# Two-layer graph network on one core: a bias row loaded later, two combines moved, and the last product banks paired anew

## The chip, the cores and the metric

The kernel runs on one core of a Trainium2 chip. The metric is the device time of one execution in microseconds. The time before is the median of three runs. Engines are named as in the profile: PE (matmul) with its weight loads PEld, DVE (vector), ACT (scalar), POOL and SP. SP and POOL issue nearly all DMAs; each issues its own in program order, and an instruction that waits holds up all that stand behind it on its engine.

## What is computed

Input x has 4096 rows of 512 columns, and adj is a 4096 x 4096 integer matrix with about one entry in 128 set. The reference, cut to what matters:

```python
# layer 0: the first 64 neighbours of each row are averaged
keep    = Ab & (cumsum(Ab, axis=1) <= 64)
nb_mean = (keep @ x) / maximum(cnt, 1)
x1 = layernorm(x + leaky_relu(x @ W_line.T + b_line)
                 + where(cnt > 0, leaky_relu(nb_mean @ W_nb.T + b_nb), 0))
# layer 1: attention over the neighbours
wh  = x1 @ W + bW
e   = leaky_relu((wh @ a1 + b1)[:, None] + (wh @ a2 + b2)[None, :], 0.2)
att = softmax(where(adj > 0, e, -9e15), axis=1)
out = layernorm(x1 + att @ wh)
```

## The kernel before, in words

Rows are worked on in 32 blocks of 128. The tile framework sets the waits between engines, but the order of the instructions on each engine is the order in which the program writes them (`tc.manual_schedule()`). A reader can thus follow each engine's queue in the code.

**Layer 0** ends with the neighbour sums: for each of 32 blocks, 64 matmuls (L509, two terms for each of 32 column blocks) into one PSUM bank. The block before is finished meanwhile by DVE in four steps, `finish(i, 0)` to `finish(i, 3)` (L468 to L487): bias and leaky relu, the sum with `own` (the rest of x1, loaded from DRAM), the layer norm with the store of x1 to DRAM, and two dot products for the attention scores. The last block, 31, is finished after the last matmul.

**Between the layers** the memory of layer 0 is reused. Three tiles `w` of 16 KB a partition are taken for layer 1. The first, `front`, holds the weights `ws` and four slots `x1s` for x1 as it is loaded. The second, `early`, takes the first three transposed blocks of x1, scratch of `finish(31)`, and own of block 31. Further up, over memory that holds the operands of layer 0's matmuls, lie `bt`, the tile `res` with the bias row `bias_w`, and the buffers `nat` of packed adjacency. Program order on SP is: four loads of `ws` (L542), the bias row broadcast to 128 partitions (L546, 256 KB), `load_turned(0..3)`, own of block 31 (L777), eight loads of `nat` for block 0 (L608), `load_turned(4..6)`. On DVE it is: `turn_x1(0..2)`, then `finish(31)`, then some small sums (L788 to L794) that POOL sends through DRAM as `e2_n` and `st_n`, which the masks need.

**The squares of wh.** For s from 0 to 31, PE makes `wh` for 128 rows with four matmuls (L809). Ahead of that, `load_turned(s)` loads x1 in four DMAs (L561) and `turn_x1(s)` transposes it in blocks of 32 on DVE (L575). The loop runs three transpositions and seven loads ahead. A load waits for the transposition that frees its slot. `finish_wh(s)` (L584) adds the bias row and writes a half of `bt`. From s = 8 (`FIRST`) on, the loop also works on the attention weights of blocks 0 and 1: `mask` (ACT L621, DVE L624), `score` (ACT L613), the largest logit (`greatest`, `shift`), and `weigh` (ACT exp, L666). Late in the loop `turn(q)` (DVE, two instructions at L685) transposes a quarter of the weights of two blocks, and `combine(q)` (four DVE sums, L698 to L701) makes the sums that a Strassen-like scheme with seven products needs. `combine_wh` (four DVE sums, L597 to L600) does this for one pair of halves of `bt`. There are 16 such pairs. The loop calls it at each s from 16 on, except at s = 22 and 26; what is left is done while the first product group runs.

**The products.** For q from 0 to 63, `consume(q)` multiplies quarter k = q mod 4 of two row blocks g = q div 4 by `bt`: seven products of four matmuls each (L724), 12.09 us a quarter. The seven results of one g lie in four PSUM tiles of one bank each, two to a bank and one alone; `where` says which. Meanwhile DVE and ACT prepare `turn` and `combine` of the next quarters and the weights of the next blocks. After a g is done, `end_low` and `end_top` add the products and `end_row` adds x1, normalizes and stores. For the last g this is written out at the end of the program: ACT copies product 1, then DVE adds 6, 2, 7, 5, 4 and 3 in this order of reading (L877 to L889). In the very last quarter the order of the products is (4, 1, 2, 6, 7, 5, 3).

Of the kernel before, what the change touches and what calls it, by code (L numbers as in the profile page):

```python
# [20 lines left out]
P = 128  # L21
# [11 lines left out]
def two_layer_adj_gnn(  # L33
# [16 lines left out]
    nc = tc.nc  # L50
# [3 lines left out]
    NT = NB // 2  # L54
# [22 lines left out]
    two, steep, far, neg_half = few[:, 0:1], few[:, 1:3], few[:, 3:4], few[:, 4:5]  # L77
# [59 lines left out]
    with ExitStack() as l0:  # L137
# [325 lines left out]
        def finish(i, g):  # L463
            if i < 0:
                return
            if g == 0:
                t = place("t")
                nc.vector.scalar_tensor_tensor(  # L468
                    t, accs.pop(i), rcnt[:, i : i + 1], bias_nb, ALU.mult, ALU.add
                )  # L470
                nc.vector.scalar_tensor_tensor(t, t, 0.01, t, ALU.mult, ALU.max)  # L471
                fin[i] = t
            elif g == 1:
                t, y = fin[i], owns.pop(i)
                nc.vector.scalar_tensor_tensor(  # L475
                    y, t, some[:, i : i + 1], y, ALU.mult, ALU.add
                )
                fin[i] = y, ln_stats(y)
            elif g == 2:
                y, stats = fin[i]  # L480
                ln_apply(y, stats)
                nc.gpsimd.dma_start(x1_blk(i), y)
            else:
                y, _ = fin.pop(i)
                for k in range(2):
                    junk = place("junk", 1)
                    nc.vector.scalar_tensor_tensor(  # L487
                        junk, y, 1.0, wa_rows[k], ALU.mult, ALU.mult,
                        accum_out=e12[:, 1 - k, i : i + 1],
                    )  # L490
# [3 lines left out]
        for s in range(NB * NS):  # L494
            i, g = divmod(s, NS)
# [10 lines left out]
            for k in range(KB):  # L506
                j = g * KB + k
# [25 lines left out]
    NP = 4  # L533
# [9 lines left out]
            ws[ts(n, SQ), :, :], w[ts(n, P), :].rearrange("(m b) c -> b m c", b=SQ)  # L543
        )
    bias_w = ep.tile([P, C], F32, name="res", bufs=1)
    nc.sync.dma_start(bias_w, b_w.partition_broadcast(P))  # L546


    bt = big.tile([P, NS // 2, 7, HC], F32, name="bt")
# [6 lines left out]
    def load_turned(s):  # L556

        if s < NS:
            part = x1_d[s // 8].rearrange("(n s a) c -> s a n c", s=8, a=SQ)[s % 8]
            for n in range(NC):  # L560
                nc.sync.dma_start(  # L561
                    x1s[ts(n, SQ), s % 4, :].rearrange("a (j c) -> a j c", c=P),
                    part[:, :, ts(n, P)],
                )

    x1ts, x1rows, pws, nats, wts, parts = {}, {}, {}, {}, {}, {}
    m4s, mms, nms, z4s, zqs, rzs, banks, sums = {}, {}, {}, {}, {}, {}, {}, {}

    FIRST = 8

    def turn_x1(s):
        if s < NS:
            t = early[:, s, :C] if s < 3 else rows.tile([P, C], F32, name="c")
            x1ts[s] = t.rearrange("p (m i) -> p m i", i=P)
            nc.vector.transpose(  # L575
                x1ts[s].rearrange("p m (j a) -> p j m a", a=SQ),
                x1s[:, s % 4, :].rearrange("p (j m b) -> p j m b", m=NC, b=SQ),
            )

    def finish_wh(s):  # L580

        kk, h = s // 8 * 4 + s % 4, s // 4 % 2
        b = bt[:, kk]
        nc.vector.tensor_tensor(  # L584
            b[:, 2 * h : 2 * h + 2, :], pws.pop(s).rearrange("p (h c) -> p h c", h=2),
            bias_w.rearrange("p (h c) -> p h c", h=2), ALU.add,
        )
        if h == 1:
            later.append(kk)
# [12 lines left out]
    def load_nat(b, h):  # L602

        if b < NB:
            nats[b, h] = ep.tile([P, 2, NS * SQ // 2], BF16, name="nat")
            rows = code_d[b].rearrange("(i a) (n x) -> n a i x", a=SQ, n=4)
            for n in range(4):
                nc.sync.dma_start(nats[b, h][ts(n, SQ)], rows[n][:, ts(h, 2), :])  # L608
# [6 lines left out]
    def mask(b, i):  # L615

        if i == 0:
            wts[b] = early if b == 0 else wp.tile([P, NI, NS * SQ], F32, name="w")
            m4s[b] = stat.tile([P, NI], F32, name="m4", bufs=2)
        w_i = wts[b][:, i, :]  # L620
        nc.scalar.activation(  # L621
            w_i, nats[b, i // 2].bitcast(U8)[:, i % 2, :], AF.Relu, bias=far, scale=-FAR
        )
        nc.vector.tensor_tensor_reduce(  # L624
            w_i, e2_n, w_i, 1.0, -3e38, ALU.subtract, ALU.max, m4s[b][:, i : i + 1]
        )
        if i % 2:
            load_nat(b + 1, i // 2)

    def score(b, i):  # L630
        w_i = wts[b][:, i, :]
        bend1(b, i, w_i, w_i)
# [16 lines left out]
    def shift(b):  # L649


        mm = mms.pop(b)
        lm = stat.tile([P, NI], F32, name="lm", bufs=2)
        for i in range(NI):
            bend1(b, i, lm[:, i : i + 1], mm[:, i : i + 1])
        nms[b] = stat.tile([P, NI], F32, name="nm", bufs=2)
        nc.vector.scalar_tensor_tensor(  # L657
            nms[b], lm, -1.0, st_n[:, :, 1, b], ALU.mult, ALU.subtract
        )
# [20 lines left out]
    def turn(q):  # L680

        g, k = divmod(q, NP)
        a = rp.tile([P, 2, 8, P], F32, name="a")
        for r in range(2):
            nc.vector.transpose(  # L685
                a[:, r].rearrange("p s (i a) -> p i s a", a=SQ),
                wts[2 * g + r][:, :, ts(k, 8 * SQ)].rearrange("p i (s x) -> p i s x", x=SQ),
            )
        if k == NP - 1:
            del wts[2 * g], wts[2 * g + 1]  # L690
        parts[q] = a

    def combine(q):
        a = parts[q]
        s = rp.tile([P, 3, 4, P], F32, name="s")
        a11, a12, a21, a22 = a[:, 0, 0:4], a[:, 0, 4:8], a[:, 1, 0:4], a[:, 1, 4:8]
        s1, s2, s4 = s[:, 0], s[:, 1], s[:, 2]
        nc.vector.tensor_tensor(s1, a21, a22, ALU.add)  # L698
        nc.vector.tensor_tensor(a21, a11, a21, ALU.subtract)
        nc.vector.tensor_tensor(s2, s1, a11, ALU.subtract)  # L700
        nc.vector.tensor_tensor(s4, a12, s2, ALU.subtract)  # L701

        parts[q] = {
            1: (a11, 0), 2: (a12, 2), 3: (s4, 3), 4: (a22, 6), 5: (s1, 4), 6: (s2, 5), 7: (a21, 1)
        }


    where = {1: (0, 0), 2: (0, 1), 4: (1, 0), 7: (1, 1), 5: (2, 0), 6: (2, 1), 3: (3, 0)}

    def consume(q):  # L710
        g, k = divmod(q, NP)
        if k == 0:
            two = [ps_s.tile([P, 2, HC], F32, name="pt")]
            two += [ps_acc.tile([P, 2, HC], F32, name="acc") for _ in range(3)]
            banks[g] = {n: two[i][:, j, :] for n, (i, j) in where.items()}
        part = parts.pop(q)


        order = (1, 2, 4, 7, 5, 6, 3) if q < NP * NT - 1 else (4, 1, 2, 6, 7, 5, 3)
        for n in order:  # L720
            lhs, rhs = part[n]
            mate = [m for m in order if where[m][0] == where[n][0]]
            for j in range(4):
                nc.tensor.matmul(  # L724
                    banks[g][n], lhs[:, j, :], bt[:, 4 * k + j, rhs, :],
                    start=(k == 0 and j == 0 and n == mate[0]),
                    stop=(k == NP - 1 and j == 3 and n == mate[-1]),
                )
# [46 lines left out]
    for s in range(4):  # L775
        load_turned(s)
    nc.sync.dma_start(owns[NB - 1], own_d[NB - 1])  # L777
    load_nat(0, 0)
    load_nat(0, 1)
    for s in range(3):  # L780
        turn_x1(s)
        load_turned(s + 4)
    for g in range(4):
        finish(NB - 1, g)

# [19 lines left out]
    for s in range(NS):  # L805
        pws[s] = ps_acc.tile([P, C], F32, name="acc")
        x1t = x1ts.pop(s)
        for m in range(NC):
            nc.tensor.matmul(  # L809
                pws[s], x1t[:, m, :], ws[:, m, :], start=(m == 0), stop=(m == NC - 1)  # L810
            )
        if s > 0:
            finish_wh(s - 1)
        turn_x1(s + 3)
        load_turned(s + 7)
        if FIRST <= s < FIRST + 8:
            b, i = divmod(s - FIRST, NI)
            mask(b, i)
            score(b, i)
        if FIRST + 4 <= s < FIRST + 12:  # L820
            b, i = divmod(s - FIRST - 4, NI)
            if i == 0:
                greatest(b)
                shift(b)
            weigh(b, i)
        if s in (FIRST + 14, FIRST + 18):
            q = (s - FIRST - 14) // 4
            turn(q)
            combine(q)
        elif s >= FIRST + 8:  # L830
            combine_wh()
    finish_wh(NS - 1)

    for q in range(NP * NT):
        g, k = divmod(q, NP)
        consume(q)
        more = 0 < q < NP * NT - 1
        if more:
# [92 lines left out]
```

## Time and profile before

| what | value |
|---|---|
| runs | 1611.77, 1612.21, 1615.34 us, median 1612.21 |
| profiled execution | 1611.63 us, of which the span is 1609.9 |
| PE / DVE / ACT / POOL busy | 98% / 82% / 56% / 16% of the span |
| layer 0's last matmul ends | 704.21 us |
| squares of wh on PE | 709.69 to 826.06 us |
| products on PE | 826.06 to about 1599.6 us |
| work after the last matmul | about 10 us |

Times in the text count from the start of the span. PE's matmul records have modelled ends and overlap by a fraction of a microsecond, so stretches of PE are best measured from start to start. In the waits, a line says which instruction waited, which one released it, the total in us, how often, and the longest. In the timeline, `x24` means that neighbouring equal instructions are merged into one row; each matmul on 32-bit data leaves two records there.

### The profile page before, as it was taken

The page shows a single profiled execution, that of the slowest core. Times are in us where ns is not written, and L with a number is a line of the kernel's source. Part 1 is how long each engine was busy: PE and PEld are TensorE (multiplying, and loading weights), DVE is VectorE, ACT ScalarE, POOL GpSimd, SP SyncE. Part 2 cuts the span into 40 slices and gives each one's busy share as a digit, 9 for nine tenths or more (in the row PEclk, how much of TensorE's full clock was granted, in tenths as well). Part 3 has the DMA queues.
Part 4 walks back from the last instruction along what each step waited for, and adds up shares of the span by engine and source line. Part 5 has one row for each costly group of instructions (what it writes and reads, how often), then busy time and mean ns, then how long its engine had stood idle before and what let it go on. Part 6 is the DMA issues. An engine that isn't in the chain of part 4 may idle for free.

```text
span 1609.9 us, 18503 instructions
## 1 busy us (share of the span) xinstructions
PE 1583.8 (98%) x6456; PEld 1221.9 (76%) x6456; DVE 1328.1 (82%) x2186; ACT 903.2 (56%) x1054; POOL 258.1 (16%) x396
## 2 busy tenths in 40 slices
PE   9999999999999999989999999999999999999997
PEld 5444448888888787854468888888888888888886
DVE  4999987999999999845798788888788888788863
ACT  2655556677676766413437655567655567655520
POOL 4455532222122222101000000000000000000000
PEclk9999999999999999999999999999999999999999
DMA  8887868767776676335211111111111111111100
GB/s 199 286 264 232 262 211 239 216 202 212 220 208 198 209 213 193 100 103 118 79 40 27 53 40 53 44 29 46 53 41 53 43 30 47 53 40 53 40 7 33
DMA packets 168365, 192.74 MB, mean 120 GB/s; under 512 B 101408, under 2 KB 134464, under 8 KB 160080
## 3 DMA queue, kind: packets, MB, share of 16 engines
q1 hardware_dynamic: 147968, 131.38, 29.6%
q0 software_dynamic: 19728, 59.27, 10.8%
q8 instruction: 50, 0.82, 0.2%
q10 hardware_dynamic: 576, 0.92, 0.2%
q14 instruction: 43, 0.35, 0.1%
HBM read 132.65 MB, written 42.08 MB: 109 GB/s over the span
## 4 chain that ended last, share of the span: by engine, by line
PE 69%; DVE 23%; DMA 3%; issue 2%; ACT 1%; POOL 1%; SPq 0%; DVEq 0%; POOLq 0%; ACTq 0%
PE acc L724 34%; PE pt L724 14%; DVE left L179 10%; PE acc L340 9%; PE acc L509 9%; PE acc L809 3%; DVE left L184 2%; DVE junk L487 2%; DVE own L475 1%; DVE st L117 1%; DVE t L471 1%; DMA a<-in_adj_dram 1%; DVE t L468 1%; DVE own L131 1%; DVE c L575 1%
## 5 line engine op out<-in xcount | busy, mean ns | idle before, releaser
L509 PE MATMUL acc<-y_hi,kt 128*128 128x512 f32 x1016 | 396.3, 390 | 2.9 <-ACT kt L249 2.9
L509 PE MATMUL acc<-y_lo,kt 128*128 128x512 f32 x1016 | 395.8, 390 | 0.0
L724 PE MATMUL acc<-bt,s 128*128 128x256 f32 x1536 | 342.1, 379 | 0.0
L724 PEld LDWEIGHTS acc<-bt,s 128*128 128x128 f32 x1536 | 292.3, 190 | 39.2
L621 ACT ACTIVATE w<-nat,few 128x1024 f32<-128x1024 uint8 x128 | 136.9, 1135 | 277.1 <-DVE a L685 237.0
L126 POOL TENSOR_TENSOR rs<-ve,few 128x1 f32<-128x1 f32 x64 | 76.1, 1190 | 1021.1 <-DVE ve L124 1021.1
L724 PE MATMUL acc<-bt,a 128*128 128x256 f32 x1024 | 231.6, 379 | 0.0
L724 PE MATMUL pt<-bt,a 128*128 128x256 f32 x1024 | 231.5, 379 | 0.0
L509 PEld LDWEIGHTS acc<-y_hi,kt 128*128 128x128 f32 x1016 | 190.7, 188 | 44.5 <-ACT kt L249 5.0
L509 PEld LDWEIGHTS acc<-y_lo,kt 128*128 128x128 f32 x1016 | 190.9, 188 | 39.3
L724 PEld LDWEIGHTS pt<-bt,a 128*128 128x128 f32 x1024 | 194.9, 190 | 26.5 <-issue 0.5
L724 PEld LDWEIGHTS acc<-bt,a 128*128 128x128 f32 x1024 | 194.9, 190 | 26.1
L685 DVE STREAM_TRANSPOSE a<-w 128x1024 f32<-128x1024 f32 x128 | 153.0, 1225 | 56.1 <-ACT w L666 53.2
L249 ACT ACTIVATE kt<-ktb,few 128x1024 fp32r<-128x1024 uint8 x124 | 139.8, 1148 | 84.7 <-PE acc L509 69.0
L167 ACT ACTIVATE edge<-a,few 128x2048 bf16<-128x2048 int32 x64 | 127.9, 1998 | 99.4 <-DVE left L184 78.0
L613 ACT ACTIVATE w<-w,st_n 128x1024 f32<-128x1024 f32 x128 | 149.4, 1234 | 49.8 <-DVE m L624 49.8
L624 DVE CUSTOM_DVE_ANT_0 w<-e_n,w 128x1024 f32<-128x1024 f32 x128 | 149.5, 1221 | 9.1 <-ACT w L621 7.7
L666 ACT ACTIVATE w<-w,nm 128x1024 f32<-128x1024 f32 x128 | 145.4, 1137 | 11.3 <-DVE nm L657 11.3
L179 DVE TENSOR_TENSOR_SCAN left<-few,edge 128x2048 bf16<-128x2048 f32 x32 | 141.3, 4416 | 12.3 <-ACT edge L167 11.2
L179 DVE TENSOR_TENSOR_SCAN left<-few,ends,edge 128x2048 bf16<-128x2048 f32 x32 | 143.2, 4476 | 0.0
L202 ACT CAST code<-left 128x2048 uint8<-128x2048 bf16 x64 | 120.6, 1884 | 7.6 <-DVE left L184 7.6
L340 PE MATMUL acc<-wt_nb,xt 128*128 128x512 f32 x256 | 115.4, 594 | 1.8 <-DVE xt L294 1.0
(135 smaller groups left out, 1528.5 us busy)
## 6 DMA issues: line engine op xcount, KB each, us to landing
a<-in_adj_dram SPq DMA_DIRECT2D x64, 1024.0 KB, 5.7
code_d<-code POOLq DMA_DIRECT2D x64, 256.0 KB, 5.2
nat<-code_d SPq DMA_DIRECT2D x256, 64.0 KB, 2.0
own_d<-xb POOLq DMA_DIRECT2D x32, 256.0 KB, 5.7
w<-x_d SPq DMA_DIRECT2D x128, 64.0 KB, 2.0
c<-in_x_dram POOLq DMA_DIRECT2D x124, 64.0 KB, 5.5
xb<-in_x_dram POOLq DMA_DIRECT2D x31, 256.0 KB, 5.7
own<-own_d SPq DMA_DIRECT2D x31, 256.0 KB, 2.7
```

What stands on the lines that cost most here:

```text
L167: nc.scalar.activation(edge_of[s], loaded.pop(s), AF.Sigmoid, bias=steep[:, 0:1], scale=STEEP, accum_out=cnts[:, h, b : b + 1],)
L179: nc.vector.tensor_tensor_scan(left, two.to_broadcast([P, CH]), e, NEIGHBORS + 2.0 if h == 0 else end, ALU.max, ALU.subtract,)
L202: nc.scalar.copy(code.bitcast(U8), seen_of.pop(s))
L249: nc.scalar.activation(kts[s], bytes_.rearrange("p t (i r) -> p t r i", r=2), AF.Sigmoid, bias=steep[:, 1:2], scale=STEEP,)
L340: nc.tensor.matmul(pl, lhs_t[:, k, :], w_t[name][:, k, :], start=(k == 0), stop=(k == NC - 1),)
L509: nc.tensor.matmul(accs[i], kt[:, k // 2, k % 2, :], term[:, j, :], start=(j == 0 and term is y_hi), stop=(j == NB - 1 and term is y_lo),)
L613: nc.scalar.activation(dst, src, AF.Prelu, bias=bias, scale=scale, alpha=0.2)
L621: nc.scalar.activation(w_i, nats[b, i // 2].bitcast(U8)[:, i % 2, :], AF.Relu, bias=far, scale=-FAR)
L624: nc.vector.tensor_tensor_reduce(w_i, e2_n, w_i, 1.0, -3e38, ALU.subtract, ALU.max, m4s[b][:, i : i + 1])
L666: nc.scalar.activation(w_i, w_i, AF.Exp, bias=nms[b][:, i : i + 1], accum_out=z4s[g][:, r, i : i + 1])
L685: nc.vector.transpose(a[:, r].rearrange("p s (i a) -> p i s a", a=SQ), wts[2 * g + r][:, :, ts(k, 8 * SQ)].rearrange("p i (s x) -> p i s x ...
L724: nc.tensor.matmul(banks[g][n], lhs[:, j, :], bt[:, 4 * k + j, rhs, :], start=(k == 0 and j == 0 and n == mate[0]), stop=(k == NP - 1 and ...
```

## The change

The bias row's load moves from ahead of all x1 loads to behind `load_turned(6)`, and the eight `nat` loads of block 0 move behind `load_turned(7)`. In the squares' loop, `turn(0)`, `combine(0)`, `turn(1)` and `combine(1)` now stand at s = 22, 24, 26 and 28; before, each turn and its combine stood together at 22 and 26. At each of these four no `combine_wh` is called, so that four of the 16 instead of two are left to the first product group. For the last g, all four quarters use the order (4, 1, 2, 6, 7, 5, 3), and the banks hold (4, 1), (2, 6), (7, 5) and (3); before they held (1, 2), (4, 7), (5, 6) and (3) for every g. On PE, POOL and ACT nothing else changes its place.

```diff
     bias_w = ep.tile([P, C], F32, name="res", bufs=1)
-    nc.sync.dma_start(bias_w, b_w.partition_broadcast(P))
...
-    where = {1: (0, 0), 2: (0, 1), 4: (1, 0), 7: (1, 1), 5: (2, 0), 6: (2, 1), 3: (3, 0)}
+    order = {True: (1, 2, 4, 7, 5, 6, 3), False: (4, 1, 2, 6, 7, 5, 3)}
+    where = {key: {n: divmod(i, 2) for i, n in enumerate(o)} for key, o in order.items()}
...
-            banks[g] = {n: two[i][:, j, :] for n, (i, j) in where.items()}
+            banks[g] = {n: two[i][:, j, :] for n, (i, j) in where[g < NT - 1].items()}
...
-        order = (1, 2, 4, 7, 5, 6, 3) if q < NP * NT - 1 else (4, 1, 2, 6, 7, 5, 3)
-        for n in order:
+        key = g < NT - 1
+        for n in order[key]:
             lhs, rhs = part[n]
-            mate = [m for m in order if where[m][0] == where[n][0]]
+            mate = [m for m in order[key] if where[key][m][0] == where[key][n][0]]
...
     nc.sync.dma_start(owns[NB - 1], own_d[NB - 1])
-    load_nat(0, 0)
-    load_nat(0, 1)
     for s in range(3):
         turn_x1(s)
         load_turned(s + 4)
+    nc.sync.dma_start(bias_w, b_w.partition_broadcast(P))
     for g in range(4):
         finish(NB - 1, g)
...
         turn_x1(s + 3)
         load_turned(s + 7)
+        if s == 0:
+            load_nat(0, 0)
+            load_nat(0, 1)
...
-        if s in (FIRST + 14, FIRST + 18):
-            q = (s - FIRST - 14) // 4
-            turn(q)
-            combine(q)
+        if s in range(FIRST + 14, FIRST + 22, 2):
+            q, part = divmod((s - FIRST - 14) // 2, 2)
+            (turn, combine)[part](q)
         elif s >= FIRST + 8:
             combine_wh()
```

## The prediction

> **What bounds the kernel now.** I read the page first, then PE's waits, then the timeline and a table of windows around the one long wait, then the end. The page says whose time counts:
>
> ```profile
> PE 1583.8 (98%) x6456; PEld 1221.9 (76%) x6456; DVE 1328.1 (82%) x2186; ACT 903.2 (56%) x1054; POOL 258.1 (16%) x396
> ```
>
> PE is busy 98% of 1609.9 us and the change removes no matmul. So a gain can only come from PE's gaps, from matmuls at a reduced clock, or from the work behind the last matmul. PE's waits (us in total, times, longest) name the gaps inside layer 1, and SP's waits name what stands behind the first:
>
> ```profile
> PE acc L809 <- DVE w L575: 5.5, 1, 5.5
> ...
> PE acc L809 <- DVE c L575: 2.6, 2, 2.2
> ```
>
> ```profile
> SPq L546 <- PE acc L509: 22.3, 1, 22.3
> ```
>
> L546 is the load of the bias row. It stood 22.3 us at the head of SP's queue until the last matmul of layer 0, because its buffer lies where PE still reads. All loads of x1 stood behind it. The timeline (start, duration, engine, line):
>
> ```profile
> 703.82 0.39 PE L509 MATMUL acc<-y_lo,kt 128*128 128x512 f32 x1
> 704.02 0.35 SPq L546 DMA_DIRECT2D res<-in_L_gnn_bW_dram  x1
> 704.41 7.56 SPq L561 DMA_DIRECT2D w<-x_d  x16
> 708.92 0.71 DVE L575 STREAM_TRANSPOSE w<-w 128x512 f32<-128x512 f32 x1 [13.01 <-DMA w<-x_d]
> ...
> 709.69 13.46 PE L809 MATMUL acc<-w 128*128 128x512 f32 x24 [5.47 <-DVE w L575]
> ```
>
> PE ends layer 0 at 704.21 and starts the first square of wh at 709.69: bias issue, first x1 load, its landing, one DVE transposition. The windows (length, busy times, then PEclk, DMA share, GB/s) show what this costs afterwards:
>
> ```profile
> 704.20:709.70 5.50, 0.03 (x2) 0.02 (x1) 0.71 (x1) 0.00 (x0) 0.00 (x0) 0.91 0.52 155
> 709.70:715.70 6.00, 6.00 (x8) 2.52 (x9) 2.75 (x4) 0.00 (x0) 0.00 (x0) 0.51 0.52 153
> 715.70:722.00 6.30, 6.30 (x16) 2.84 (x15) 5.31 (x16) 1.15 (x2) 1.74 (x3) 1.00 0.58 170
> ...
> 779.00:784.40 5.40, 3.16 (x9) 1.14 (x7) 3.91 (x14) 4.64 (x11) 0.00 (x0) 1.00 0.17 49
> ```
>
> For 6 us after the wait PE ran at half clock; after the shorter gap near 782 it did not. The busy share hides this: slow matmuls count as busy.
>
> [...]
>
> **Part one: the bias row moves behind load_turned(6).** The changed program's list of waits, as built, gives three facts. The x1 loads of squares 0 to 3 carry no wait for PE; they follow the four loads of w, issued from 679.99 to 681.84. At 0.47 us each (7.56 / 16) they leave by 689.4 and land some 15 us before 704. The wait for the last L509 is now carried by the load of own 31 (L777), the next DMA on SP. The first transposition waits for that matmul too, as before, since its target lies over layer 0's buffers.
>
> So the gap doesn't vanish: one transposition remains in it. From 708.92 to PE's start is 0.77 us, and DVE can start at about 704.2 (the previous block's L468 started at 689.75, the recorded end of its last matmul, estimated from the 14.45 us of a block). PE starts at 704.21 + 0.77 = 704.98, instead of 709.69: **4.7 us** (bounds 4.4 to 4.9). The idle stretch is 0.8 us, less than the 2.5 us after which the clock stayed at 1.00. A square takes 3.43 us at full clock (transpositions at 733.48, 736.91, 740.35 follow PE). The first three took 722.98 - 709.69 = 13.29 instead of 10.30: another **3.0 us** (bounds 0 to 3.0; I take all of it).
>
> Now the queues behind it. SP from 704.05: own (0.38), twelve x1 loads for squares 4 to 6 (5.7 us, to 710.2), bias (0.35). By 3.6 us to land for both: own is there at 707.7, bias at 714. DVE: three transpositions to 706.1, L468 and L471 to 707.5, L475 when own is there, then 5.28 us (715.73 to 721.01) to turn_x1(3), which ends at 713.7. PE needs it at 704.98 + 10.3 = 715.3, its weights 0.4 sooner: slack 1.2 us. If own took 5.8, the slowest own load of late layer 0, PE would lose 1.0. The bias row is first read by finish_wh(0), next on DVE; ahead of turn_x1(4) it can be 3 us late before PE (square 4 at 718.7) sees it. SP then issues square 7, the eight nat loads (4.58 us) that moved behind it, and square 8, landing near 725 and needed at 732. Block 0's first mask is due near 737, nat is there by 722, and e2_n starts 8 us sooner than before. These moves I cost at 0, their cover being these slacks.
>
> **Part two: combine(0) and combine(1) move two squares behind their turn, and two more combine_wh fall behind the loop.** Inside the squares PE waits for DVE three times:
>
> ```profile
> 774.48 3.60 PE L809 MATMUL acc<-w,c 128*128 128x512 f32 x8
> 778.41 3.70 PE L809 MATMUL acc<-w,c 128*128 128x512 f32 x8 [0.34 <-DVE c L575]
> 784.35 41.87 PE L809 MATMUL acc<-w,c 128*128 128x512 f32 x96 [2.24 <-DVE c L575]
> ```
>
> By start times squares 19 and 20 lose 0.5 and 2.5 us. ACT and DVE hand block 1's masks, scores and weights to each other there, one square taking 4.7 us (772.95, 777.66) instead of 3.43. The change starts later, at square 22: 3.0 us stay. The 96 records from 784.35 should take 41.2 us and L724 starts after 41.7: 0.5 us at square 30, whose transposition ended at 819.03 after DVE had worked without a pause. Ahead of it the change takes away combine(1) (815.07 to 817.73, 2.7 us) and one combine_wh (1.6 us), so **0.5 us** goes (bounds 0 to 0.5). Afterwards four combine_wh instead of two (838.16 to 841.34) stand ahead of turn(2). DVE's total to there is the same, and it enters the products about 3 us less behind, so I put turn(2) within 0.5 us of its old place. combine(2) ended at 846.48 and group 2 starts at 850.23: 3.7 us cover. Cost 0; without that lead, 3.2 us, still covered.
>
> **Part three: the banks of the last four product groups.** Same 28 products per group, so PE's time is the same. The end before:
>
> ```profile
> 1598.14 0.42 DVE L877 TENSOR_TENSOR c<-c,acc 128x256 f32<-128x256 f32 x1 [19.49 <-PE acc L724]
> 1598.59 0.42 DVE L878 TENSOR_TENSOR c<-c,pt 128x256 f32<-128x256 f32 x1
> 1598.93 0.41 DVE L879 TENSOR_TENSOR c<-c,acc 128x256 f32<-128x256 f32 x1
> ```
>
> L877 reads product 6, finished at 1594.4, but waits for its bank mate 5, finished at 1597.9. Paired as (4,1), (2,6), (7,5), (3), L877 and L878 run three microseconds before and L879 waits for (7,5) at the same moment as L877 did. DVE's tail starts with L879: 1598.93 - 1598.14 = **0.8 us**. Nothing takes its place: product 3 ends near 1599.6 and is read at 1603. Product 7 is now fifth, so turn(62) waits 1.7 us longer for its buffer (1558.37 becomes 1560.1) and ends at 1562.5, before combine(62) at 1563.55, which waits for PE anyway: 0.
>
> **Sum.** 4.7 + 3.0 + 0.5 + 0.8 = 9.0 us. The profiled execution took 1611.63 us (span 1609.9 and 1.7 around it): 1602.6. The median of the runs is 0.6 above it: **1603.2 us**.
>
> **Rivals.** (a) *The clock falls all the same*: 6.0 us gained, 1606.2. [...] Against: clock 1.00 after 2.5 us. (b) *DVE's short way to square 3 fails*, own landing late: about 1.0 us lost, 1604.2. (c) *The move does not free the loads*, if something else holds SP from 682 to 704: only 0.5 + 0.8, 1610.9. Against: w's loads did leave at 679.99. (d) *Slower: the wait is moved, not removed.* Bias now stands behind own and twelve loads; finish_wh(0) holds DVE until it lands, and turn_x1(4) stands behind. From 717 on each microsecond of lateness is one of PE's. Landing at 725 would give an 8 us stall, with the cold clock 3 more: 11 us against 9.0 won, and from about 727 the kernel is over 0.2% slower, say 1616. Against: no load of this kind took over 6.4 us near there, and bias would need 16. (e) *More gain*: the 3.0 us at squares 19 and 20 shrink too, 1600.2. Nothing in the change touches them.
>
> **How the numbers follow.** A measurement can tell about 0.2%, 3.2 us, from no change. Forecast 0.73, (a) 0.08, (b) 0.07, (c) 0.04, (d) 0.03, (e) 0.05. All but (c) and (d) are faster by more than 3.2 us: faster 0.93, same 0.04, slower 0.03. The range runs from the forecast less 2.2 (half of (e) and the scatter of medians) to just past (a): 1601.0 to 1606.6.
>
> **What would show it.** Right: sixteen x1 loads on SP between 682 and 690; PE's wait ahead of the first square 0.8 us, PEclk 1.00 behind it; L724 starting near 817.9 instead of 826.06; waits at squares 19 and 20 still there, that at 30 gone; the second tail sum starting before the last products end. Wrong: a PEclk of 0.5 near 705 to 711 (a), a wait for DVE at square 3 (b) or 4 with DVE waiting for bias (d), SP idle from 682 to 704 (c).

## The result, and the profile after

| what | before | after |
|---|---|---|
| runs | median 1612.56 us (1611.77 to 1615.34, 6 runs) | median 1605.32 us (1603.85 to 1608.79, 6 runs) |
| profiled execution / its span | 1611.63 / 1609.9 us | 1603.85 / 1602.1 us |
| end of layer 0 on PE | 704.21 us | 705.39 us |
| squares, start to start of the products | 709.69 to 826.06 us | 706.02 to 819.11 us |
| start of products to end of span | 783.8 us | 783.0 us |

The ratio is 0.9956 with an interval of 0.9943 to 0.9969: faster, by 7.2 us (5.0 to 9.2). The forecast was 1603.2 us; the median lies 2.1 us above it and inside the range. Lines of the changed program are one lower than before in the first two parts of layer 1: the squares are L808, the transposition of x1 L574, the load of x1 L560; at the end of the program they are one higher.

PE's list of waits (us in total, times, longest). The 5.5 us are down to 0.6; the two waits at squares 19 and 20 stand as they did:

```profile
PE acc L808 <- DVE c L574: 2.6, 2, 2.2
...
PE acc L808 <- DVE w L574: 0.6, 1, 0.6
```

The timeline of SP (start, duration, engine, line), around the end of layer 0:

```profile
681.42 1.85 SPq L542 DMA_DIRECT2D w<-in_L_gnn_W_dram  x4
683.31 9.87 SPq L560 DMA_DIRECT2D w<-x_d  x16
705.23 0.34 SPq L777 DMA_DIRECT2D w<-own_d  x1
706.00 6.54 SPq L560 DMA_DIRECT2D w<-x_d  x12
712.58 0.43 SPq L781 DMA_DIRECT2D res<-in_L_gnn_bW_dram  x1
```

Sixteen loads of x1 now leave right behind those of w, 21 us earlier. The wait for layer 0 is carried by own (L777), which is issued at 705.23 where it was 712.06 before. The bias row (L781) is issued 8.6 us later than before. The timeline of PE and then the windows (length, busy times of PE, PEld, DVE, ACT, POOL, then PEclk, DMA share, GB/s):

```profile
705.00 0.39 PE L509 MATMUL acc<-y_lo,kt 128*128 128x512 f32 x1
706.02 10.57 PE L808 MATMUL acc<-w 128*128 128x512 f32 x24 [0.64 <-DVE w L574]
716.43 55.10 PE L808 MATMUL acc<-w,c 128*128 128x512 f32 x128
771.87 3.70 PE L808 MATMUL acc<-w,c 128*128 128x512 f32 x8 [0.34 <-DVE c L574]
777.80 41.47 PE L808 MATMUL acc<-w,c 128*128 128x512 f32 x96 [2.23 <-DVE c L574]
819.11 3.62 PE L724 MATMUL pt<-bt,a 128*128 128x256 f32 x16
```

```profile
706.02:712.00 5.98, 5.97 (x14) 2.77 (x15) 5.02 (x10) 0.00 (x0) 0.56 (x1) 1.00 0.46 142
```

The clock stays at 1.00 behind the short gap (0.64 us), and the first three squares take 716.43 - 706.02 = 10.41 us; they took 13.29. From the start of the last row of squares to the products it is 819.11 - 777.80 = 41.31 us, where it was 826.06 - 784.35 = 41.71: the delay at square 30 is gone. From the end of layer 0 to the first product it was 826.06 - 704.21 = 121.85 us and is 819.11 - 705.39 = 113.72: 8.1 us, where the first two parts of the sum were put at 8.2. The end, on DVE:

```profile
1587.73 0.42 DVE L878 TENSOR_TENSOR c<-c,acc 128x256 f32<-128x256 f32 x1 [16.03 <-PE acc L724]
1588.18 0.42 DVE L879 TENSOR_TENSOR c<-c,acc 128x256 f32<-128x256 f32 x1
1591.12 0.42 DVE L880 TENSOR_TENSOR c<-c,acc 128x256 f32<-128x256 f32 x1 [2.52 <-PE acc L724]
```

Two sums now run before the last matmuls have ended, and only the third waits for them. The last sixteen records of PE and the last normalization on DVE, before and then after:

```profile
1596.15 3.62 PE L724 MATMUL acc<-bt,s 128*128 128x256 f32 x16
1606.12 0.73 DVE L131 TENSOR_SCALAR c<-c,mv,rs 128x256 f32<-128x256 f32 x2 [0.44 <-POOL rs L126]
```

```profile
1589.20 3.62 PE L724 MATMUL acc<-bt,s 128*128 128x256 f32 x16
1598.33 0.73 DVE L131 TENSOR_SCALAR c<-c,mv,rs 128x256 f32<-128x256 f32 x2 [0.44 <-POOL rs L126]
```

From start to start it was 1606.12 - 1596.15 = 9.97 us, and is 1598.33 - 1589.20 = 9.13: 0.8 us.

### The profile page after: what moved, and what is told of

The parts are those of the page before. It is cut to its first block, busy times and chain, and to the rows that moved or that the text cites. A ratio compares the mean times of both kernels' runs of the same rounds, so it can differ in the third digit from the quotient of the medians.

```text
span 1602.1 us, 18501 instructions
## 1 busy us (share of the span) xinstructions
PE 1580.6 (99%) x6456; PEld 1218.9 (76%) x6456; DVE 1327.9 (83%) x2186; ACT 902.8 (56%) x1054; POOL 258.7 (16%) x396
## 4 chain that ended last, share of the span: by engine, by line
PE 71%; DVE 21%; DMA 3%; issue 3%; ACT 1%; POOL 1%; SPq 0%; POOLq 0%; DVEq 0%; ACTq 0%
PE acc L724 34%; PE pt L724 14%; DVE left L179 10%; PE acc L340 9%; PE acc L509 8%; PE acc L808 5%; DVE left L184 2%; DVE junk L487 2%; DVE own L475 1%; DVE st L117 1%; DVE t L471 1%; DMA a<-in_adj_dram 1%; DVE t L468 1%; DVE own L131 1%; DMA a<-in_L_gnn_W_line_dram 1%
## 5 line engine op out<-in xcount | busy, mean ns | idle before, releaser
L249 ACT ACTIVATE kt<-ktb,few 128x1024 fp32r<-128x1024 uint8 x124 | 139.7, 1148 | 84.6 <-PE acc L509 66.9
```

What stands on the lines that cost most here:

```text
L249: nc.scalar.activation(kts[s], bytes_.rearrange("p t (i r) -> p t r i", r=2), AF.Sigmoid, bias=steep[:, 1:2], scale=STEEP,)
```

## The experiments

The kernel before was run again beside each group of experiments. Its median was 1612.2 us in the first comparison, 1614.1 and 1614.3 us in the later ones, so across the groups only ratios can be compared, not times.

**The parts alone.** Three kernels make one part of the change each, with the kernel before as base. The edit of `p1_bias` is:

```diff
-    nc.sync.dma_start(bias_w, b_w.partition_broadcast(P))
...
-    load_nat(0, 0)
-    load_nat(0, 1)
...
         load_turned(s + 4)
+    nc.sync.dma_start(bias_w, b_w.partition_broadcast(P))
...
+        if s == 0:
+            load_nat(0, 0)
+            load_nat(0, 1)
```

> Only the loads on SP are moved (bias row behind load_turned(6), block 0's nat loads behind load_turned(7)); the rest is the kernel before. Theory: nearly all of the change is here. PE starts the first square about 0.6 us after layer 0's last matmul instead of 5.5, its clock stays at 1.00 (3.0 us), so the products start 7.6 us earlier after the end of layer 0; the wait at square 30 (0.5 us) stays, since DVE's order is the old one; the end is the old one. Total 7.6 us faster, ratio 0.9953. Rival (the three parts share the gain about equally, or DVE's waits eat part one): less than 5 us.

Measured: 1605.45 us (5 runs) against 1612.2 (33 runs), ratio 0.9957 (0.9943 to 0.9971). The timeline of PE at the end of layer 0, in the last row of squares and at the first product:

```profile
703.75 0.39 PE L509 MATMUL acc<-y_lo,kt 128*128 128x512 f32 x1
...
776.56 41.87 PE L807 MATMUL acc<-w,c 128*128 128x512 f32 x96 [2.23 <-DVE c L574]
818.27 3.62 PE L723 MATMUL pt<-bt,a 128*128 128x256 f32 x16
```

Layer 0 ends at 704.14 and the products start at 818.27, 114.13 us against 121.85: 7.7 us, the 4.7 + 3.0 of the first part. The moved loads are most of the change. The bias row and the code loads were not moved one without the other.

`p2_comb` moves the combines alone, the last hunk of the change:

```diff
-        if s in (FIRST + 14, FIRST + 18):
-            q = (s - FIRST - 14) // 4
-            turn(q)
-            combine(q)
+        if s in range(FIRST + 14, FIRST + 22, 2):
+            q, part = divmod((s - FIRST - 14) // 2, 2)
+            (turn, combine)[part](q)
```

> Only turn and combine of the first two quarters are moved apart; loads and banks are those before. Theory: the wait for DVE at square 30 goes and nothing else: 0.5 us faster, ratio 0.9997, not to be told from 1 by the time; turn(2) about 1.3 us later after the start of the products, with no wait of PE for it. Rival (the four combine_wh left over delay the first groups): a wait of PE for DVE in the first four quarters and 1 to 3 us slower.

Measured: 1612.48 us (13 runs), ratio 0.9997 (0.9989 to 1.0005), less than runs can tell. The last squares and the first product on PE:

```profile
786.48 41.47 PE L809 MATMUL acc<-w,c 128*128 128x512 f32 x96 [2.23 <-DVE c L575]
827.79 3.62 PE L724 MATMUL pt<-bt,a 128*128 128x256 f32 x16
```

This stretch is 827.79 - 786.48 = 41.31 us against 41.71: 0.4 us, and the row is the same in the changed kernel. From the end of layer 0 (706.49) to the products it is 121.30 us, 0.55 less than before, but 0.15 of that is not the edit's: the first three squares, which stand ahead of it, took 13.11 us at their slow clock and not 13.29.

`p3_banks` takes the orders and banks of the last group alone:

```diff
-    where = {1: (0, 0), 2: (0, 1), 4: (1, 0), 7: (1, 1), 5: (2, 0), 6: (2, 1), 3: (3, 0)}
+    order = {True: (1, 2, 4, 7, 5, 6, 3), False: (4, 1, 2, 6, 7, 5, 3)}
+    where = {key: {n: divmod(i, 2) for i, n in enumerate(o)} for key, o in order.items()}
```

> Only order and banks of the last four quarters are changed. Theory: from the start of the last quarter to the end of the span 0.8 us less (two tail sums run before the last products end), all before that as in the kernel before; ratio 0.9995. Rival (another sum or the last product becomes the limit): less than 0.3 us in that stretch.

Measured: 1612.3 us (13 runs), ratio 0.9997 (0.9988 to 1.0005). The last records of PE and the last normalization:

```profile
1596.33 3.62 PE L725 MATMUL acc<-bt,s 128*128 128x256 f32 x16
1605.57 0.74 DVE L131 TENSOR_SCALAR c<-c,mv,rs 128x256 f32<-128x256 f32 x2 [0.44 <-POOL rs L126]
```

That is 1605.57 - 1596.33 = 9.24 us against 9.97: 0.7 us. The three traced gains are 7.7 + 0.4 + 0.7 = 8.8 us, where the whole change has 9.0: within 0.2 us they add. Parts two and three are shown by the traces alone, since the times can't tell them from nothing.

**The clock alone** (`warm`). In the kernel before, PE is kept busy during the wait for x1:

```diff
+        if s == 0:
+            warm = ps_acc.tile([P, C], F32, name="acc")
+            for _ in range(6):
+                nc.tensor.matmul(warm, ws[:, 0, :P], ws[:, 1, :], start=True, stop=True)
```

> The kernel before, all loads as before, with six extra matmuls on the weights of wh (128x128x512, 32 bit, 0.86 us each, results not used) that PE makes between layer 0 and the first square, while it waits. Theory (the slow first six microseconds are PE's clock after the idle stretch): clock 1.00 in the first squares, the wait itself still there, products 3.0 us earlier, ratio 0.9981. Rival (the first matmuls are slow because sixteen loads run into SBUF beside them): the loads are the same, so the first squares stay slow and the time is the same or longer.

Measured: 1612.71 us (13 runs), ratio 1.0002 (0.9994 to 1.001). The expected 3.0 us did not come. The timeline of PE and its windows (these as above):

```profile
704.59 5.31 PE L809 MATMUL acc<-w 128*128 128x512 f32 x12
709.88 10.57 PE L813 MATMUL acc<-w 128*128 128x512 f32 x24
722.38 56.90 PE L813 MATMUL acc<-w,c 128*128 128x512 f32 x128 [1.94 <-DVE c L575]
```

```profile
709.70:713.00 3.30, 3.30 (x9) 1.45 (x9) 0.83 (x2) 0.00 (x0) 0.00 (x0) 1.00 0.40 107
...
718.00:720.00 2.00, 2.00 (x6) 0.76 (x4) 1.18 (x4) 0.00 (x0) 0.74 (x2) 1.00 0.49 141
...
723.00:724.00 1.00, 1.00 (x3) 0.43 (x2) 1.00 (x2) 0.00 (x0) 0.74 (x2) 0.50 0.70 176
```

The dummies do keep the clock at 1.00, and the first three squares take 10.4 us, although the same sixteen loads run beside them: the loads were not what made these squares slow. But then PE waits 1.94 us for the transposition of square 3, and the clock falls behind that wait: 128 records in 56.9 us instead of 55.1. What was saved is given back. In the kernel before, that transposition ran from 721.01 and PE, slowed by the clock, came for it at 722.98; a PE at full speed would have come at 709.69 + 10.30 = 719.99. The transposition ended at 721.71, so of the 3.0 us of slow clock only some 1.3 (722.98 - 721.71) were PE's own, and the rest lay over DVE's work on block 31. The reading is that in the changed kernel the 3.0 us are won in full only because DVE's way to square 3 has moved up too.

**Own behind the x1 loads** (`ownlate`). That reading is put to the test by holding DVE's way back in the changed kernel:

```diff
-    nc.sync.dma_start(owns[NB - 1], own_d[NB - 1])
     for s in range(3):
         turn_x1(s)
         load_turned(s + 4)
+    nc.sync.dma_start(owns[NB - 1], own_d[NB - 1])
```

> The changed kernel with the load of own 31 put behind the twelve x1 loads instead of ahead of them; the bias row stays behind both. Theory: the gain of the change rests on VectorE's way to square 3 having moved up with TensorE, which own's place on SyncE's queue sets. Own is now issued near 711.3 instead of 705.2 and lands near 714.9; from own's landing to the end of square 3's transposition VectorE took 6.1 us in the kernel before, so it ends near 720.9, where TensorE wants it at 716.4: a wait of 4.5 us, and half clock for 3.3 us behind it (1.7 us lost). Expected 4.5 to 6.2 us more than the changed kernel: 1611 (1609.8 to 1611.5), ratio to before 0.999. Rival (own's landing is not what the first VectorE chain waits for): no wait at square 3, 1605.3.

Measured: 1613.34 us (20 runs) against 1614.3 (39 runs), ratio 0.9991 (0.9984 to 0.9998): nearly all of the gain is gone, although PE starts the squares as early as in the changed kernel. The timeline of DVE, then of PE:

```profile
718.67 0.75 DVE L475 SCALAR_TENSOR_TENSOR w<-w,e 128x512 f32<-128x512 f32 x1 [6.71 <-DMA w<-own_d]
...
723.96 0.70 DVE L574 STREAM_TRANSPOSE c<-w 128x512 f32<-128x512 f32 x1
```

```profile
709.48 10.57 PE L808 MATMUL acc<-w 128*128 128x512 f32 x24 [0.64 <-DVE w L574]
724.72 58.01 PE L808 MATMUL acc<-w,c 128*128 128x512 f32 x128 [4.67 <-DVE c L574]
```

DVE waits 6.71 us for own, PE 4.67 for DVE (4.5 expected), and the 128 records behind take 58.01 us instead of 55.1: 2.9 us of slow clock, where 1.7 were expected. The two are 7.6 us, more than the 6.2 that were expected at most; from the end of layer 0 (708.85) to the products (830.32) it is 121.47 us against 113.72.

**The bias row still later** (`late`). Rival (d), made real in the changed kernel:

```diff
-    nc.sync.dma_start(bias_w, b_w.partition_broadcast(P))
...
             load_nat(0, 1)
+            nc.sync.dma_start(bias_w, b_w.partition_broadcast(P))
```

> The changed kernel with the bias row's load moved on, behind the eight code loads of square 0: rival (d) of the prediction made real. Theory: the bias row is issued near 724 and lands near 727.9; the first addition of the bias holds VectorE until then and the transposition of square 4 stands behind it, so that TensorE, which wants square 4 at 719.9, waits some 9.5 us, and then runs at half clock for about 6 us (3 us lost): 12.5 us more than the changed kernel, 1617.8 (range 1614 to 1619), slower than the kernel before. TensorE's list of waits shows one wait of 8 to 10 us on L574. Rival (VectorE's queue is not held, or the row lands sooner, since the loads ahead issue faster): under 4 us more, 1609 or less.

Measured: 1616.97 us (20 runs), ratio 1.0018 (1.0012 to 1.0025): slower than the kernel before. DVE and PE in the timeline:

```profile
728.50 0.69 DVE L583 TENSOR_TENSOR bt<-acc,res 128x512 f32<-128x512 f32 x1 [13.20 <-DMA res<-in_L_gnn_bW_dram]
729.10 0.70 DVE L574 STREAM_TRANSPOSE c<-w 128x512 f32<-128x512 f32 x1
```

```profile
729.86 53.85 PE L807 MATMUL acc<-w,c 128*128 128x512 f32 x120 [9.08 <-DVE c L574]
```

The row lands near 728.5, where layer 0 ended at 706.14. Taken back to the 704.21 of the prediction, that is 726.6; its rule "from 717 on each microsecond is one of PE's" gives 9.6 us, and 9.08 are there. The clock falls as well: the 120 records take 53.85 us, where 120/128 of 55.10 are 51.66, a loss of 2.2 us (3 expected). In all it is 125.15 us to the products, 11.4 more than in the changed kernel (12.5 expected). Eight code loads on SP's queue lie between a gain and a loss.

**What is left to gain, and the scatter** (`again`, `relu`, `swap`, `both`). `again` is the changed kernel unaltered. `relu` splits `mask` in two: `hide` is its relu on ACT with the load of the next codes, `largest` its running maximum on DVE.

```diff
-            mask(b, i)
+            if s == FIRST:
+                hide(b, i)
+            largest(b, i)
...
+            if s < FIRST + 7:
+                hide(*divmod(s - FIRST + 1, NI))
```

`swap` exchanges the places of the weights' buffers, so that the first transpositions write over nothing that layer 0's last matmul reads:

```diff
-    wp = tile_p("l1_w", 3)
+    wps = [tile_p(f"l1_w{k}", 1) for k in range(3)]
...
-    front = wp.tile([P, NI, NS * SQ], F32, name="w")
-    early = wp.tile([P, NI, NS * SQ], F32, name="w")
+    front = wps[0].tile([P, NI, NS * SQ], F32, name="w")
+    early = wps[1].tile([P, NI, NS * SQ], F32, name="w")
...
-            wts[b] = early if b == 0 else wp.tile([P, NI, NS * SQ], F32, name="w")
+            wts[b] = early if b == 0 else wps[(b + 1) % 3].tile([P, NI, NS * SQ], F32, name="w")
```

`both` has the two together.

> The changed kernel once more, unaltered, beside the next three. My theory: its traced gain is 9.0 us, but executions of one kernel differ by steps of about 1.6 us because TensorE's clock falls for 3.3 us after a wait of 1.8 to 2.2 us in some of them and not in others; the first six runs fell to 1603.9 once and to 1605.2 to 1608.8 five times. Expected over more runs: median 1604.5 to 1605.5, lowest 1602.7 to 1603.9, ratio to before 0.9950 to 0.9957, and each 0.001 of mean granted clock worth about 1.6 us. Rival (the traced gain is an artefact of one lucky execution, and something of the change costs 1.5 us in most runs): lowest stays at 1603.8 and the whole cluster stands at 1605.3.

> The changed kernel with one alteration: in the loop of squares ScalarE makes the next mask's relu (and the code load that goes with it is issued) ahead of the present exp, so that VectorE's running maximum no longer waits for a relu that stands behind an exp. Theory: the two waits of TensorE at squares 19 and 20 (0.34 and 2.23 us) come from the hand-over between ScalarE and VectorE of 4.7 us per square; with the relu ahead a round takes about 3.75 us, and both waits go: 3.0 us by start times, and with the 2.2 us wait gone the clock can no longer fall there. Expected 1602.3, ratio to the unaltered changed kernel 0.9981 (gain 2.2 to 4.6 us). Rival (ScalarE's or VectorE's own work per square is the limit, not the hand-over): waits stay, gain 0 to 0.5 us. Second rival (the relu delays an exp that VectorE's sum needs): TensorE waits more, up to 2 us slower.

> The changed kernel with one alteration: the three buffers of the weights change places, so that the target of the first transpositions no longer lies over buffers that the last matmul of layer 0 reads. The transpositions and the load of own 31 can then run ahead of the end of layer 0. Theory: the rest of the gap between layer 0 and the first square (1.02 us between starts where 0.23 is the pace, 0.64 us shown as a wait) is the single transposition behind the last matmul; it goes, 0.6 to 0.8 us, TensorE runs through. Own 31 is there before it is needed and square 3's transposition ends some 1 us earlier. Expected ratio to the unaltered changed kernel 0.9996 (within what runs can tell; the trace decides: no wait of TensorE for L574 ahead of the first square). Rival (the accumulator of the first square or the weights hold the first square as well): the wait stays 0.3 us or more with another releaser.

> The changed kernel with both alterations (relu ahead of the exp, buffers of the weights exchanged). Theory: they touch different waits and add: 3.0 + 0.7 = 3.7 us, 1601.6 against 1605.3, ratio to before 0.9933, ratio to the unaltered changed kernel 0.9977. TensorE has no wait left between the end of layer 0 and the first product. Rival (they share a cover, e.g. VectorE early in the squares): the sum is below 3 us.

Measured, beside 9 runs of the kernel before with a median of 1614.11 us:

| kernel | median (range), 5 runs each | ratio to before | layer 0's end to first product |
|---|---|---|---|
| again | 1606.13 (1604.66 to 1606.99) | 0.9949 (0.9935 to 0.9962) | 707.66 to 821.38: 113.7 |
| relu | 1601.74 (1601.57 to 1602.26) | 0.9924 (0.9912 to 0.9936) | 706.22 to 816.82: 110.6 |
| swap | 1605.57 (1604.94 to 1607.87) | 0.9950 (0.9938 to 0.9963) | 708.64 to 823.13: 114.5 |
| both | 1602.30 (1601.81 to 1603.68) | 0.9928 (0.9916 to 0.9941) | 707.38 to 817.08: 109.7 |

`relu` beats both kernels, by 4.4 us in the median against `again` and 3.1 us in the trace. The timeline of DVE in the changed kernel, then in `relu`, shows why. One round of a square, from maximum to maximum, takes 764.64 - 759.93 = 4.71 us with 2.26 of waiting, and then 766.09 - 762.51 = 3.58 with 1.12:

```profile
759.93 1.23 DVE L623 CUSTOM_DVE_ANT_0 w<-e_n,w 128x1024 f32<-128x1024 f32 x1 [2.21 <-ACT w L620]
...
764.64 1.23 DVE L623 CUSTOM_DVE_ANT_0 w<-e_n,w 128x1024 f32<-128x1024 f32 x1 [2.26 <-ACT w L620]
```

```profile
762.51 1.23 DVE L628 CUSTOM_DVE_ANT_0 w<-e_n,w 128x1024 f32<-128x1024 f32 x1 [1.13 <-ACT w L620]
...
766.09 1.23 DVE L628 CUSTOM_DVE_ANT_0 w<-e_n,w 128x1024 f32<-128x1024 f32 x1 [1.12 <-ACT w L620]
```

PE has no wait left at squares 19 and 20; all squares from the fourth on are one row of its timeline:

```profile
717.25 99.73 PE L815 MATMUL acc<-w,c 128*128 128x512 f32 x232
```

`swap` does away with the 0.6 us gap (the first square starts at 708.48, 0.23 us after the last record of layer 0 does), but its profiled execution lost 1.7 us to the clock instead, behind a wait that the changed kernel has as well; its times can't be told from those of `again`. A row of its PE timeline and one of its windows:

```profile
780.13 43.16 PE L808 MATMUL acc<-w,c 128*128 128x512 f32 x96 [2.22 <-DVE c L574]
```

```profile
781.50:783.00 1.50, 1.50 (x3) 0.53 (x2) 1.50 (x4) 0.44 (x2) 0.00 (x0) 0.50 0.48 135
```

The same 96 records took 41.47 us in the changed kernel after a wait of 2.23 us. `both` came to 3.8 us less than `again` in the median and 4.0 in the trace, as its two parts together should (3.7 expected); against `relu` alone the trace shows 0.9 us and the medians show no gain.

Layer 0 has such a place too, a wait of 1.8 us for ACT's L249 near 614. PE's timeline and one window there, in the changed kernel and then in `again`, which is the same program:

```profile
614.38 0.50 PE L509 MATMUL acc<-y_hi,kt 128*128 128x512 f32 x1 [1.83 <-ACT kt L249]
...
616.00:617.00 1.00, 1.00 (x6) 0.82 (x5) 1.00 (x2) 0.42 (x1) 0.00 (x0) 1.00 0.99 369
```

```profile
615.07 0.50 PE L509 MATMUL acc<-y_hi,kt 128*128 128x512 f32 x1 [1.82 <-ACT kt L249]
...
616.00:617.00 1.00, 1.00 (x4) 0.80 (x3) 0.93 (x3) 1.00 (x2) 0.00 (x0) 0.50 0.93 319
```

In the profiled executions of `p2_comb`, `again`, `swap` and `ownlate` half clock for about 3.4 us followed this wait (in `p2_comb` the clock was 0.54, 0.50, 0.50 and 0.76 in the four microseconds from 615 on). In six of the other eight (before, after, `p1_bias`, `relu`, `both`, `late`) the clock was 1.00 there; in `warm` and `p3_banks`, whose mean clocks are 0.997 and 0.996, the place itself is not shown. So a part of the scatter goes with whether the clock falls behind short waits. Of the eleven runs of the changed kernel (six and `again`), three show a mean clock of 0.998 (mean time 1604.5 us), six 0.997 (1605.9) and two 0.996 (1607.9). The five runs of `relu`, which has no wait of 2.2 us at square 20, all show 0.998 and lie within 0.7 us. But `both` lacks that wait as well, and three of its five runs show 0.997. Nor is the clock the only source: in the six profiles with clock 1.00 behind 614, layer 0, whose code is the same in all, ends anywhere between 704.1 and 707.4 us.

## Why the prediction was right

**Part one.** 4.7 us of waiting: the gap between layer 0's last recorded end and the first square was 5.48 us and is 0.63, 4.85 us less. 3.0 us of clock: 13.29 became 10.41, 2.9 us. Right, with one correction that `warm` and `ownlate` show. The two terms were written as two independent gains, and the second one isn't: it needs square 3 to be ready at full speed. The prediction did follow DVE's queue to square 3 and found a slack of 1.2 us to the load of the weights on PE; 1.5 was there (the transposition ended at 714.54, the weights were loaded at 716.00). But it priced the failure of that path (rival b) by the wait alone, 1.0 us for an own that lands 2.2 us late. In `ownlate` own is issued 7 us later against the end of layer 0, the wait is 4.67 us, and the clock adds 2.9 to it. What a wait of 1.0 us at this place does to the clock no run shows.

**The queues behind.** The first sixteen x1 loads took 9.87 us on SP, not 7.56, and had left by 693.2, not 689.4; with 12 us still to go to the end of layer 0 that cost nothing. Own was there when DVE came for it at 708.55. The bias row landed later than reckoned: twelve x1 loads took 6.54 us, not 5.7, and DVE waited:

```profile
716.41 0.69 DVE L583 TENSOR_TENSOR bt<-acc,res 128x512 f32<-128x512 f32 x1 [1.87 <-DMA res<-in_L_gnn_bW_dram]
```

The transposition of square 4 behind it ended at 717.7 and PE started that square at 719.86. The eight code loads took 7.67 us on SP instead of 4.58, and DVE waited 5.20 us for x1 of square 8; PE came to it only at 733.6, and did not wait. Block 0's first codes were there at 724.5, when ACT's wait for them ended, not by 722; that is still ahead of the first mask on DVE at 737.86. The covers held: behind the 1.87 us for the bias row 2.1 us were left, behind the 5.20 for square 8 some 2.7.

**Parts two and three.** 0.5 and 0.8 us were forecast; 0.4 was measured for the one, alone and in the changed kernel, and 0.7 (alone) and 0.8 for the other. The 0.5 reckoned the last row of squares at 41.2 us at full pace; it takes 41.31. The second transposition of the products came 1.3 us later after their start than before, where 0.5 was forecast; PE didn't wait.

**The sum and the median.** 8.13 + 0.84 = 8.97 us in the trace, as forecast (9.0). The step that was off is the last: "The median of the runs is 0.6 above it". The profiled execution of after came out 1.2 us above the forecast 1602.6, since its layer 0, which the change doesn't touch, ended 1.2 us later, in the waits for its first loads. And the median stands 1.5 us above that execution, not 0.6, because, by their mean clocks, most runs had a clock fall that the profiled one escaped. Of the 9.0 us, the two comparisons of medians show 7.2 (5.0 to 9.2) and 8.0 (0.9935 to 0.9962 of 1614.1, that is 6.1 to 10.5); both hold 9.0. The part that the falls have in the 7.2 is not shown. Where 33 runs of the kernel before were taken, 13 lie below its most frequent clock of 0.996, while 8 of the 11 runs of the changed kernel lie below its best, 0.998; beside `again` it is 7 of 9 before and 3 of 5 after, and there the medians are 8.0 us apart. How often the clock falls thus differs from one comparison to the next, and why stays open.

**The rivals.** (a) was argued away with "clock 1.00 after 2.5 us". `swap` shows that this was one outcome of two: after the same wait (2.22 us in PE's timeline) the clock was 0.50 from 781.5 to 783. After the 0.64 us that are left ahead of the first square no trace shows a fall: `p1_bias` and after stood at 1.00 there, and in after, `again`, `relu`, `ownlate` and `late` the 24 records behind the gap took 10.57 us each time. (c) is out, as sixteen loads left between 683.3 and 693.2. (d) had the right mechanism and nearly the right price (`late`). (e) was open to another change (`relu`), not to this one.

## What to carry to other kernels

A load that waits for its buffer delays all that stand behind it in its queue (in the kernel before one waited 22.3 us, with sixteen behind it): move it behind the loads that are needed sooner, and reckon from its first reader until when it may land, since a few loads too far cost more than was won (eight loads in `late`: 11.4 us). A stretch of slow clock is worth what it costs only if the next stage is ready for a fast engine (in `warm` the first squares ran at full clock, and the ratio was 1.0002), so follow the other engine's queue to the first point where they meet. Shorten waits of about 2 us even where the profiled execution shows full clock behind them: in other executions here such a wait cost 1.7 us more.

## What the runs showed of the hardware

Waits of PE of 1.8 to 2.2 us were followed by half clock in some executions (`p2_comb`, `again`, `swap`, `ownlate`, `warm`) and by full clock in others. At L249, after 1.83 and 1.82 us, the changed kernel and `again`, the same program, show one each: 1.00 and 0.50 between 616 and 617. When the clock fell after such a wait, it stayed down about 3.4 us, a loss of 1.7 us (`swap`) or 1.8 (`warm`). After waits of 4.7, 5.5 and 9.1 us the loss was 2.9, 3.0 and 2.2 us (`ownlate`, before, `late`). After 0.64 us the clock stayed at 1.00 (after, `p1_bias`). Why it falls behind a wait of about 2 us in one execution and not in another is not shown by any run.
